# Forming a head's symmetric products once: 48 of 64 columns, three products by q, and every second head's sums begun on GpSimd

## The chip, the cores and the metric

The kernel runs on one core of a Trainium2 chip. A core has TensorE (PE, matrix products into PSUM, with weight loads PEld beside them), VectorE (DVE), ScalarE (ACT), GpSimd (POOL) and SyncE (SP, which issues DMAs). Each engine works through its own queue in order; semaphores join them. The time is device microseconds of one execution, and the median of several runs counts: 831.38 us for the kernel before (three runs, 828.76 to 834.36).

## The reference

Two transformer layers over x of 16 batches, 128 rows and 256 columns, float32, with a context of the same shape. The change touches only the first part of the first layer. For each batch, of 128 channels in 16 heads of 8 and a sequence of 256:

```python
kv = einsum('bhil,bhjl->bijhl', k_, v_)          # k_ and v_ are both the context
y = irfft(rfft(kv) * rfft(ssm_kernel))[..., :L]  # a causal convolution along l
out = y + kv * D
out = einsum('bijhl,bhil->bjhl', out, q_)        # q_ is the normed x
x = x + tanh(g_xattn[0]) * out
```

As k_ and v_ are the same tensor, kv of a head is symmetric in i and j, and so is its convolution. After it come a mixture of 8 experts beside a shared one, causal attention on the context, and a mixture of 32 experts, each added to x behind a layer norm.

## The kernel before

The convolution is done as matrix products with Toeplitz matrices. The 16 batches are two halves of 8 (`HALF`). The sequence of 256 lies on the 128 partitions in two blocks (`KC`). For a half i and a head h (16 of them, `SSM_H`), `convolve` does four things:

1. GpSimd forms `kv` (L331): for 2 blocks x 8 batches the 8 x 8 products of the head's rows, 1,024 elements a partition, in one of 2 buffers.
2. TensorE multiplies with the head's Toeplitz blocks `toe` into `y` in PSUM (L339): three matmuls of 512 columns, of block 0 for output block 0, and of both blocks for output block 1. A float32 matmul goes as two instructions, so there are six passes a head. `y` takes two of the eight PSUM banks and has 3 buffers; the two others are for transposes (`tr`).
3. VectorE multiplies `y` by the normed and transposed x, `qT` (L347), into `pr`, with i innermost (2 buffers).
4. VectorE sums over i into `qT` (L353), in the place of the head's own q.

After 16 heads TensorE transposes `qT` back (L358, tile `to`) and VectorE adds it to x (L360). The layer norm of a half is `prepare`: statistics per tile (L184, L187), the root on ScalarE (L189), its reciprocal (L190), the normalisation (L211, here with the columns reversed), transposes (L214) and a copy by ScalarE into `qT` (L216). That of the second half is woven into the heads of the first from head 6 on, held back until the product of head 5 (`meanwhile`, L362).

Behind the convolution comes the first mixture: `norm` and `choose` for chunks of four tiles (statistics again by L184 to L190, tiles `st_f`, `mv_f`, `rs_f`; rows by L211; transposes, copies `xT_f` by L216; router logits L391; Exp on ScalarE L441; the best two of 8 by L405 to L417), the shared expert (L617 into `pg` and `pu`, L431 to L433, L669 into `os`, opened by a zero product L660), then `place0` and the sends of rows to DRAM by GpSimd (L725), which are held in step with the shared expert (`paced`).

The order within each engine's queue is not the order of the source lines: the tile framework plans it when the kernel is built, by its own costs, from what each instruction needs and which buffer it takes. So a change of one stage can move instructions of the next to other places. ScalarE loads a table of functions when it changes between Sqrt, Exp and Tanh.

Of the kernel before, what the change touches and what calls it, by code (L numbers as in the profile page):

```python
# [10 lines left out]
F32 = mybir.dt.float32  # L11
# [4 lines left out]
ALU = mybir.AluOpType  # L16
AX = mybir.AxisListType

P = 128
# [8 lines left out]
TOK = CH * P  # L28

SSM_H, SSM_I = 16, 8  # L30
HALF = B // 2
# [22 lines left out]
def flamingo(ctx: ExitStack, tc: tile.TileContext, a: dict, out: bass.AP):  # L54
    nc = tc.nc
    V, S, G, T = nc.vector, nc.scalar, nc.gpsimd, nc.tensor
# [7 lines left out]
    def bank(tag, name, bufs):  # L64
        return banks[-1].tile([P, 512], F32, tag=tag, name=name, bufs=bufs)
# [127 lines left out]
    def down_from_end(t):  # L193

        return t.rearrange("p (c t) -> p c t", c=KC)[:, :, ::-1]
# [26 lines left out]
    with (  # L222
# [15 lines left out]
        for _ in range(WARM):  # L238
# [3 lines left out]
                rhs=zeros_b.unsqueeze(1).to_broadcast([P, 4, P]),  # L242
# [16 lines left out]
        for i in range(SSM_H // 4):  # L259
            at = taps[4 * i, :]  # L260
# [19 lines left out]
        at = KC * 2 * SH0 * P  # L280
# [39 lines left out]

        def convolve(i, qT, between):

            n = KC * HALF
            full = [P, n, SSM_I, SSM_I]
            q, c = (t.rearrange("p k b t -> p (k b) t") for t in (qT, cT[i]))
            for h in range(SSM_H):
                if h in between:
                    between[h](last)
                hs = slice(h * SSM_I, (h + 1) * SSM_I)
                kv = cv.tile([P, n, SSM_I, SSM_I], F32, tag="kv", name=f"kv{i}_{h}", bufs=2)  # L330
                G.tensor_tensor(  # L331
                    kv, c[:, :, hs].unsqueeze(3).to_broadcast(full), c[:, :, hs].unsqueeze(2).to_broadcast(full), ALU.mult
                )
                t = toe[h // 4][:, h % 4]
                y = cv_psum.tile([P, KC * TOK], F32, tag="y", name=f"y{i}_{h}", bufs=3)
                for lb in range(KC):
                    for kc in range(lb + 1):
                        off = P - (lb - kc) * P
                        T.matmul(  # L339
                            y[:, lb * TOK : (lb + 1) * TOK],  # L340
                            lhsT=t[:, off : off + P],
                            rhs=kv[:, kc * HALF : (kc + 1) * HALF].rearrange("p b i j -> p (b i j)"),
                            start=(kc == 0),
                            stop=(kc == lb),
                        )
                pr = cv.tile(full, F32, tag="pr", name=f"pr{i}_{h}", bufs=2)
                last = V.tensor_tensor(  # L347
                    pr,
                    y.rearrange("p (b i j) -> p b j i", b=n, i=SSM_I),
                    q[:, :, hs].unsqueeze(2).to_broadcast(full),  # L350
                    ALU.mult,
                )
                V.tensor_reduce(q[:, :, hs], pr, AX.X, ALU.add)  # L353
            for j in range(HALF):
                b = i * HALF + j
                tp = bank("tr", f"to{b}", 2)
                for lb in range(KC):
                    T.transpose(tp[:, lb * P : (lb + 1) * P], qT[:, lb, j, :], ident)  # L358
                x = xs[b].rearrange("p (c t) -> p c t", c=KC)
                V.scalar_tensor_tensor(x, down_from_end(tp[:, :D]), tg_x[:, 0:1], x, ALU.mult, ALU.add)  # L360
# [7 lines left out]
        tg_h = base.tile([P, 1], F32, tag="tg_h", name="tg_h")  # L368
        qTs = [prepare(0)]
        convolve(0, qTs[0], {6: meanwhile})  # L370
        convolve(1, qTs[1], {})

    banks.append(ctx.enter_context(tc.tile_pool(name="psum", bufs=2, space=bass.MemoryType.PSUM)))
# [634 lines left out]
    def attention():  # L1008


        chunks, sends = [], []
        for b in range(CHUNKS[-1][0]):
            if any(b == b0 for b0, _ in CHUNKS):
                steps = []
                chunks.append(steps)
            for now, before in [(0, None), (None, 2), (1, None), (None, 3), (None, 4)]:
                if now is not None:
                    steps.append(lambda b=b, i=now: part(b, i))
                elif before is not None and b > 0:
                    steps.append(lambda b=b, i=before: part(b - 1, i))  # L1020
                else:
                    continue
                if sends:
                    steps.append(sends.pop(0))
            for g in range(len(GROUPS)):
                if b > 0 and GROUPS[g][1] == b:
                    sends += dispatch(g)
        return chunks, sends
# [37 lines left out]
    chunks, left = attention()  # L1066
# [251 lines left out]
```

## Time and profile before

| | us |
|---|---|
| median of 3 runs | 831.38 |
| the profiled execution | 832.41 |
| its span, first to last instruction | 830.6 |
| convolution: first product by q to last sum over i | 21.43 to 110.25 |
| first mixture up to the first row sent | 110.3 to 137.81 |
| share of the span: PE, PEld, DVE, ACT, POOL | 85%, 60%, 65%, 44%, 40% |
| granted TensorE clock, mean | 0.919 of full speed |

A group's row in the profile reads: line, engine, operation, tiles, partitions x elements, count; then busy time in us and the mean of one in ns; then the engine's idle time before it and what ended it. A row of the timeline reads: start, length, engine, line, operation; in brackets the idle time before it and what ended that. [...] A row of a stretch gives its bounds and length, then busy time and number of instructions of PE, PEld, DVE, ACT and POOL, the granted clock, the DMA share and GB/s.

### The profile page before, as it was taken

The numbers are of one execution on the slowest core, as the hardware profiler recorded it, in microseconds if no ns is written. First come the engines' busy times: TensorE is split into PE (matmuls) and PEld (weight loads), VectorE is DVE, ScalarE is ACT, GpSimd is POOL, SyncE is SP. The second block draws the span as 40 slices with busy tenths as digits, with TensorE's granted clock in tenths as the row PEclk, the third lists the DMA queues.
The fourth block names the chain that finished last, engine by engine and source line by source line (L and its number), as shares of the span: only waits on it lengthen the run. The fifth ranks groups of instructions, "written<-read, shape, count | busy, mean of one in ns | idle before, by whom it ended". The sixth has DMA issues, their size and how long they took to land.

```text
span 830.6 us, 12160 instructions
## 1 busy us (share of the span) xinstructions
PE 703.4 (85%) x3928; PEld 496.4 (60%) x3928; DVE 541.2 (65%) x1579; ACT 367.6 (44%) x811; POOL 332.9 (40%) x326
## 2 busy tenths in 40 slices
PE   6999979989999799999969989958867999788820
PEld 3444445567775577656547747735546898677720
DVE  5999995335446754568667874685883555476756
ACT  2110037115322666652356354426524777566624
POOL 3756702300516100012272057007462677766640
PEclk8999978999999999999979987969987999999975
DMA  8999996122442233541143034063125676788575
GB/s 266 327 371 274 269 262 166 58 72 83 154 131 83 64 102 106 132 116 30 46 124 65 13 89 118 15 164 113 67 100 190 210 228 190 247 291 262 187 244 180
DMA packets 134016, 128.97 MB, mean 155 GB/s; under 512 B 42976, under 2 KB 117888, under 8 KB 133824
## 3 DMA queue, kind: packets, MB, share of 16 engines
q1 hardware_dynamic: 120704, 91.61, 39.5%
q0 software_dynamic: 13152, 36.52, 12.3%
q8 instruction: 32, 0.52, 0.3%
q14 instruction: 32, 0.26, 0.1%
q10 hardware_dynamic: 96, 0.05, 0.0%
HBM read 64.23 MB, written 63.92 MB: 154 GB/s over the span
## 4 chain that ended last, share of the span: by engine, by line
PE 46%; DVE 25%; DMA 10%; issue 7%; ACT 6%; POOL 3%; ACTq 1%; SPq 1%; DVEq 0%; POOLq 0%
PE y L339 7%; DMA part<-parts 4%; PE gu L782 4%; PE eo L1209 3%; PE sc L858 3%; PE pu L617 3%; PE pg L617 3%; PE eh L1197 3%; DVE mn L869 3%; PE eo L792 2%; PE pt L882 2%; PE os L669 2%; ACT ex L875 2%; PE avT L896 2%; PE lg_r L391 2%
## 5 line engine op out<-in xcount | busy, mean ns | idle before, releaser
L978 POOL DMA_INDIRECT sent<-row,dst x96 | 94.0, 979 | 123.8 <-DVE dst L609 94.3
L1234 POOL DMA_INDIRECT parts<-ey,to x114 | 111.6, 979 | 58.9 <-issue 23.2
L875 ACT ACTIVATE ex<-sc,mn 128x128 f32<-128x128 f32 x256 | 71.6, 385 | 68.0 <-DVE mn L869 67.9
L812 POOL DMA_INDIRECT part<-parts,places x32 | 31.2, 975 | 144.6 <-DVE rd L912 88.8
L339 PE MATMUL y<-kv,toe 128*128 128x512 f32 x192 | 85.0, 597 | 0.0
L1209 PE MATMUL eo<-wt,ehs 128*128 128x256 f32 x228 | 62.0, 403 | 17.4 <-DVE ehs L1207 17.3
L331 POOL TENSOR_TENSOR kv<-cT 128x1024 f32<-128x1024 f32 x32 | 60.6, 1893 | 38.0 <-PE y L339 33.2
L725 POOL DMA_INDIRECT sent<-row,places x32 | 31.2, 976 | 103.5 <-DVE places L504 38.2
L1187 ACT COPY wt<-wts 128x512 f32 x114 | 66.3, 620 | 13.9 <-issue 8.6
L617 PE MATMUL pg<-xT_s,wts 128*128 128x512 f32 (+1 forms) x160 | 66.3, 535 | 1.9 <-DVE silu L432 1.9
L1197 PE MATMUL eh<-xts,wt 128*128 128x128 f32 x456 | 64.7, 286 | 2.8 <-ACT wt L1187 2.8
L1197 PEld LDWEIGHTS eh<-xts,wt 128*128 128x128 f32 x456 | 62.2, 201 | 8.2 <-ACT wt L1187 4.1
L617 PE MATMUL pu<-xT_s,wts 128*128 128x512 f32 (+1 forms) x160 | 63.7, 517 | 1.9 <-DVE hs L433 1.9
L669 PE MATMUL os<-wts,hs 128*128 128x256 f32 x256 | 65.0, 387 | 0.0
L339 PEld LDWEIGHTS y<-kv,toe 128*128 128x128 f32 x192 | 36.0, 192 | 41.2 <-issue 29.1
L669 PEld LDWEIGHTS os<-wts,hs 128*128 128x128 f32 x256 | 48.4, 194 | 15.7 <-issue 9.7
L1209 PEld LDWEIGHTS eo<-wt,ehs 128*128 128x128 f32 x228 | 40.9, 197 | 25.2 <-DVE ehs L1207 20.7
L1192 DVE COPY xts<-xt 128x512 f32<-128x512 f32 x57 | 38.7, 686 | 25.5 <-PE xt L1190 18.7
L869 DVE TENSOR_REDUCE mn<-sc 128x4 f32<-128x512 f32 x64 | 41.6, 684 | 20.3 <-PE sc L858 20.0
L782 PEld LDWEIGHTS gu<-xts,wt 128*128 128x128 f32 x368 | 46.4, 196 | 8.6 <-DVE xts L776 4.8
L782 PE MATMUL gu<-xts,wt 128*128 128x128 f32 x368 | 49.2, 283 | 1.9 <-DVE xts L776 1.8
L1218 ACT COPY ey<-eo 128x512 f32<-128x512 f32 x57 | 33.4, 586 | 33.7 <-PE eo L1209 29.3
(250 smaller groups left out, 1360.0 us busy)
## 6 DMA issues: line engine op xcount, KB each, us to landing
sent<-keys SPq DMA_DIRECT2D x1, 17018.0 KB
got<-sent SPq DMA_DIRECT2D x19, 804.0 KB, 5.0
part<-parts SPq DMA_DIRECT2D x48, 256.0 KB, 4.7
sent<-keys SPq DMA_DIRECT2D x2, 2944.0 KB
got<-sent SPq DMA_DIRECT2D x22, 256.0 KB, 3.0
parts<-ey SPq DMA_DIRECT2D x22, 256.0 KB, 2.1
wts<-in_sw SPq DMA_DIRECT2D x3, 1024.0 KB, 11.8
wts<-in_w SPq DMA_DIRECT2D x3, 1024.0 KB
```

The lines of the kernel that those rows point to most:

```text
L331: G.tensor_tensor(kv, c[:, :, hs].unsqueeze(3).to_broadcast(full), c[:, :, hs].unsqueeze(2).to_broadcast(full), ALU.mult)
L339: T.matmul(y[:, lb * TOK : (lb + 1) * TOK], lhsT=t[:, off : off + P], rhs=kv[:, kc * HALF : (kc + 1) * HALF].rearrange("p b i j -> p (b i ...
L617: T.matmul(ps, lhsT=w(kc), rhs=xT[:, kc, :n], start=(kc == 0), stop=(kc == KC - 1))
L669: T.matmul(o[:, k * D : (k + 1) * D], lhsT=hs[j][:, t * P : (t + 1) * P], rhs=wC[:, j, :], start=False, stop=(j == SH0 - 1 and k == len(ts ...
L782: T.matmul(gu[:, half * D + u * P : half * D + (u + 1) * P], lhsT=wt[:, u, w : w + P], rhs=xt[:, u * D + kc * P : u * D + (kc + 1) * P], s ...
L869: least = V.tensor_reduce(mn[:, 4 * r : 4 * r + 4], scs[r].rearrange("p (h t) -> p h t", t=P), AX.X, ALU.min)
L875: S.activation(ex[:, i, :], scs[r][:, at : at + P], AF.Exp, bias=mn[:, i : i + 1], scale=-1.0)
L978: ins = G.indirect_dma_start(out=sent[:, :], out_offset=bass.IndirectOffsetOnAxis(ap=dst[:, t, k : k + 1], axis=0), in_=row, in_offset=None,)
L1187: S.copy(wt[:, i], wts[:, bass.ds(offsets[u % GRP], W1_ROW)])
L1197: T.matmul(eh[:, i * P : (i + 1) * P], lhsT=wt[:, i, cols], rhs=xt[:, i * D + kc * P : i * D + (kc + 1) * P], start=(kc == 0), stop=(kc == ...
L1209: T.matmul(eo[:, i * D : (i + 1) * D], lhsT=h[:, i * P : (i + 1) * P], rhs=wt[:, i, KC * P :], start=True, stop=True,)
L1234: ins = G.indirect_dma_start(out=parts[:, :], out_offset=bass.IndirectOffsetOnAxis(ap=to[:, t % GRP : t % GRP + 1], axis=0), in_=y[:, t % ...
```

## The change

With m = 4, the 8 x 8 products of a head fall into four blocks of 4 x 4. The block of low j and high i is the mirror of that of high j and low i, so 48 products hold all 64. `kv` now has 48 elements for each block and batch, made by two GpSimd instructions of 512 and 256 elements (all 8 rows by the high 4; the low 4 by the low 4), in 4 buffers. The matmuls take 384 columns and write 48 of every 64 columns of `y`. VectorE multiplies by q in three instructions of 512, 256 and 256 elements, the last reading the mirrored block with i and j exchanged, into a full `pr` (4 buffers). For odd heads GpSimd adds the high half of i onto the low half in `pr` (512 elements), and VectorE sums over four i in place of eight. The sum over i of a head is issued behind the products of the next head (`sums`, `add_up`).

```diff
@@ -320,37 +320,68 @@
 
         def convolve(i, qT, between):
 
             n = KC * HALF
+            m = SSM_I // 2
             full = [P, n, SSM_I, SSM_I]
             q, c = (t.rearrange("p k b t -> p (k b) t") for t in (qT, cT[i]))
+            sums = []
+            def add_up():
+                V.tensor_reduce(*sums.pop(0), AX.X, ALU.add)
             for h in range(SSM_H):
                 if h in between:
                     between[h](last)
                 hs = slice(h * SSM_I, (h + 1) * SSM_I)
-                kv = cv.tile([P, n, SSM_I, SSM_I], F32, tag="kv", name=f"kv{i}_{h}", bufs=2)
-                G.tensor_tensor(
-                    kv, c[:, :, hs].unsqueeze(3).to_broadcast(full), c[:, :, hs].unsqueeze(2).to_broadcast(full), ALU.mult
-                )
+                kv = cv.tile([P, n, 3 * m * m], F32, tag="kv", name=f"kv{i}_{h}", bufs=4)
+                k, k0, k1 = (c[:, :, hs][:, :, part] for part in (slice(0, 2 * m), slice(0, m), slice(m, 2 * m)))
+                for at, left, right in [(0, k, k1), (2 * m * m, k0, k0)]:
+                    size = [P, n, left.shape[2], m]
+                    G.tensor_tensor(
+                        kv[:, :, at : at + size[2] * m].rearrange("p b (j i) -> p b j i", i=m),
+                        left.unsqueeze(3).to_broadcast(size),
+                        right.unsqueeze(2).to_broadcast(size),
+                        ALU.mult,
+                    )
                 t = toe[h // 4][:, h % 4]
                 y = cv_psum.tile([P, KC * TOK], F32, tag="y", name=f"y{i}_{h}", bufs=3)
                 for lb in range(KC):
                     for kc in range(lb + 1):
                         off = P - (lb - kc) * P
                         T.matmul(
-                            y[:, lb * TOK : (lb + 1) * TOK],
+                            y[:, lb * TOK : (lb + 1) * TOK].rearrange("p (b s) -> p b s", b=HALF)[:, :, : 3 * m * m],
                             lhsT=t[:, off : off + P],
-                            rhs=kv[:, kc * HALF : (kc + 1) * HALF].rearrange("p b i j -> p (b i j)"),
+                            rhs=kv[:, kc * HALF : (kc + 1) * HALF],
                             start=(kc == 0),
                             stop=(kc == lb),
                         )
-                pr = cv.tile(full, F32, tag="pr", name=f"pr{i}_{h}", bufs=2)
-                last = V.tensor_tensor(
-                    pr,
-                    y.rearrange("p (b i j) -> p b j i", b=n, i=SSM_I),
-                    q[:, :, hs].unsqueeze(2).to_broadcast(full),
-                    ALU.mult,
+                pr = cv.tile(full, F32, tag="pr", name=f"pr{i}_{h}", bufs=4)
+                yb = y.rearrange("p (b s) -> p b s", b=n)
+                y01, y00 = (
+                    yb[:, :, at : at + size].rearrange("p b (j i) -> p b j i", i=m)
+                    for at, size in [(0, 2 * m * m), (2 * m * m, m * m)]
                 )
-                V.tensor_reduce(q[:, :, hs], pr, AX.X, ALU.add)
+                low, high = slice(0, m), slice(m, 2 * m)
+                for out_j, out_i, src in [
+                    (slice(0, 2 * m), high, y01),
+                    (low, low, y00),
+                    (high, low, y01[:, :, low, :].rearrange("p b j i -> p b i j")),
+                ]:
+                    dst = pr[:, :, out_j, out_i]
+                    by = q[:, :, hs][:, :, out_i].unsqueeze(2).to_broadcast(list(dst.shape))
+                    last = V.tensor_tensor(dst, src, by, ALU.mult)
+                if h % 2:
+                    G.tensor_tensor(pr[:, :, :, low], pr[:, :, :, low], pr[:, :, :, high], ALU.add)
+                    pr = pr[:, :, :, low]
+                sums.append((q[:, :, hs], pr))
+                if len(sums) > 1:
+                    add_up()
+            while sums:
+                add_up()
             for j in range(HALF):
                 b = i * HALF + j
                 tp = bank("tr", f"to{b}", 2)
```

## The prediction

> **What bounds the kernel now.** I first cut the span by stage: the convolution runs from 21.4 us (first product on VectorE) to 110.3 us (end of its last reduction). The table of busy time by stretch, columns PE, PEld, DVE, ACT, POOL, then clock and DMA:
>
> ```profile
> 21.40:66.00 44.60, 43.16 (x112) 19.35 (x111) 43.90 (x58) 4.29 (x9) 30.29 (x16) 1.00 1.01 343
> 66.00:110.30 44.30, 40.69 (x107) 18.43 (x106) 43.57 (x59) 0.20 (x1) 26.50 (x14) 1.00 1.11 269
> 110.30:138.00 27.70, 25.34 (x99) 16.16 (x100) 23.28 (x130) 14.84 (x22) 0.19 (x1) 0.69 0.92 223
> ```
>
> TensorE and VectorE are both nearly full for 88.9 us, GpSimd is not (64%). Which one sets the pace is read from the groups of this stage:
>
> ```profile
> L339 PE MATMUL y<-kv,toe 128*128 128x512 f32 x192 | 85.0, 597 | 0.0
> L331 POOL TENSOR_TENSOR kv<-cT 128x1024 f32<-128x1024 f32 x32 | 60.6, 1893 | 38.0 <-PE y L339 33.2 <-DMA cT<-in_ctxT 4.1 <-POOL kv L331 0.7
> L347 DVE TENSOR_TENSOR pr<-y,qT 128x1024 f32<-128x1024 f32 x32 | 38.6, 1213 | 5.6 <-PE y L339 5.1
> L353 DVE TENSOR_REDUCE qT<-pr 128x128 f32<-128x1024 f32 x32 | 38.1, 1208 | 0.2
> ```
>
> and from GpSimd's own order of time:
>
> ```profile
> 26.62 1.89 POOL L331 TENSOR_TENSOR kv<-cT 128x1024 f32<-128x1024 f32 x1 [0.68 <-PE y L339]
> 29.19 1.89 POOL L331 TENSOR_TENSOR kv<-cT 128x1024 f32<-128x1024 f32 x1 [0.68 <-PE y L339]
> 31.77 1.89 POOL L331 TENSOR_TENSOR kv<-cT 128x1024 f32<-128x1024 f32 x1 [0.68 <-PE y L339]
> ```
>
> The reader is to see that the products of a head start every 2.575 us and each waits 0.68 us for TensorE. The chain of waits agrees: long pieces of L339 (one of 46 matmuls, 19.76 us). 2.575 us is six passes of 0.429 us. VectorE issues L347 and L353 back to back at 1.13 us each (53.44 to 55.70 for two), so it needs 2.26 of every 2.575 us, and the layer norm of the second half (statistics, eight normalisations) and the eight updates of x eat the rest. So TensorE leads by only 12%, and VectorE is the second wall.
>
> **The change, two heads at a time** (an even and an odd one).
>
> TensorE: 12 passes over 384 in place of 512 columns. Passes of 512 go at 0.429, of 256 (L669, 8 in 1.73) at 0.216, so 384 is 0.322 and two heads take 3.87 against 5.15. Weight loads (0.19) stay hidden. The output now has gaps (48 used, 16 not), which no row shows. [...] I take 0.322, since 47 of 48 steps are contiguous. [...] At 0.429 the sum below would turn from a gain into about 5 us of loss.
>
> VectorE: intervals, not durations, count. 1024 elements take 1.13, 512 take 0.60 (L433 at 133.50, the next at 134.10), so 1.04 ns an element and 0.07 for each instruction; 256 take 0.33 (eight L211 rows, 115.57 to 118.15: 0.32 each). Products: 2 x (0.60 + 0.33 + 0.33) = 2.52 in place of 2.26, as two more instructions a head cost 0.13. Sums: 1.13 for the even head, 0.60 for the odd one, in place of 2.26. Together 4.25 against 4.52. [...] Patterns: L347 already reads y with a step of eight elements at the rate of L353, which reads without gaps, so runs of four get no surcharge. Its upper bound is L417, 1.464 us for 768 elements with a step of 32, against 0.950 for L607 without: 1.54 times.
>
> GpSimd: 1024 take 1.893, memsets of 16, 128, 512 take 0.12, 0.20, 0.517, so about 0.1 is fixed. 512 is 1.00, 256 is 0.55, kv of a head 1.55. The add of the odd head (512, both inputs full tensors) no row shows: below 0.52 (memset), above 1.54 x 1.00; I take 1.1, nearest to the 512 piece. Two heads: 2 x 1.55 + 1.1 = 4.2 against 3.79.
>
> So the three need 3.87, 4.25 and 4.2 where TensorE alone set 5.15. VectorE becomes the bound, with GpSimd 0.05 behind it.
>
> Sum for the stage. VectorE's work from first product to last reduction: 32 x 1.26 = 40.3, 16 x 1.73 = 27.7, and what stays there from the profile, 11.0 (statistics 3.1 and 0.35, normalisations 4.5 with their waits, eight x at 0.39). That is 79.0. Its start comes 0.65 earlier (six passes shorter by 0.107), at 20.8. The added wait: the reduction of an odd head h waits for GpSimd's add, and behind it in VectorE's queue stand the products of head h+2, which free the y buffer for TensorE's head h+5. In the built order the add stands behind the kv of head h+5, which waits for y of head h+1. The loop is 1.93 + 1.55 + 1.1 + 0.60 + 1.26 = 6.4 us for four heads where VectorE needs 8.5, so it does not set the pace; walking the queues head by head leaves 1.7 us of single late adds. At the very end the add (1.1) lies beside the reduction of head 14 (1.13). The stage ends at 20.8 + 79.0 + 1.7 = 101.5 in place of 110.25: **8.7 us earlier**. Four buffers instead of two are free in time.
>
> [...]
>
> ```profile
> 9.54 1.52 DVE L188 TENSOR_SCALAR rs_conv<-mv_conv 128x8 f32<-128x8 f32 x1
> 11.05 1.91 DVE L91 CAST causal_b<-causal 128x128 bf16<-128x128 f32 x1
> 9.08 1.89 POOL L331 TENSOR_TENSOR kv<-cT 128x1024 f32<-128x1024 f32 x1 [4.09 <-DMA cT<-in_ctxT]
> 10.98 1.90 POOL L331 TENSOR_TENSOR kv<-cT 128x1024 f32<-128x1024 f32 x1
> ```
>
> Two tiny instructions last until a GpSimd product ends. Products and reductions never do (1.17 to 1.22). GpSimd now works on to 15 us, beside the first normalisations, but in pieces half as long: I take nothing, with 0.7 either way.
>
> What moves. In the built order the statistics of the first half's tiles (L184, L187) no longer lie between heads: seven of eight ran from 85.5 to 109; now all stand behind the last reduction. ScalarE's second Sqrt table load, which came after the copies of the second chunk, now comes before them:
>
> ```profile
> 120.89 1.09 ACT L216 ACTIVATE xT_f<-tp_f 128x512 f32<-128x512 f32 x2 [0.29 <-PE tp_f L214]
> 122.00 1.28 ACT L189 ACT_TABLE_LOAD   x1
> 123.29 0.20 ACT L189 ACTIVATE rs_f<-rs_f 128x4 f32<-128x4 f32 x1
> ```
>
> Counted from the last reduction: the first chunk's logits come at 8.1 as before, since TensorE's opening of `os` (L660) still waits for the last x. Then Exp, the root of the first chunk's scores at 10.35, Sqrt load to 11.6, two roots to 12.05, and only then rows 4 to 7, between the pieces of the top-2 (12.4 to 14.1; before at 6.6). Their copies end at 15.3 (before 11.7), those of xT_s at 17.0 (14.2), and the logits L391 of chunk 1, on the path, start at 16.4 in place of 13.8: **2.6 us lost**, 0.5 to 4 with the reordering's doubt. Two table loads fewer later on gain nothing, as silu waits for PE there.
>
> From 138 us on SP's, GpSimd's and, but for a few places, all orders are the same, and the sends are paced by the layer beside them, so the rest shifts whole. The 17 MB fill of `sent` is through before the earlier first send (131.7): the SP queue gets on at 123.85.
>
> Sum: -8.7 + 2.6 = -6.1 us on an execution of 832.41 (span 830.6), so 826.3. That execution is 1.03 above the median 831.38; against the median it is **825.3**.
>
> **Rivals.** (1) GpSimd becomes the bound mildly, its pieces 1.05 to 1.19 times my price. For: 4.2 stands beside 4.25, and runs of four are unseen there. Two heads then take up to 5.0: the stage gains 2.4 to 6, the total lies at 828.5 to 832.5. (2) Slower: the same place beyond that point. From 1.19 times (5.0) on, 16 pairs gain less than the 2.6 lost; at 1.3 times, 5.46 a pair, the stage is 16 x 0.31 = 5.0 longer and the time 831.4 + 5.0 + 2.6 = 839; at the bound of 1.54 times 855. Against: 1.893 us hold to 0.01 for all 32. Passes at 0.429 end at 836 too. (3) Better: the reordering costs 0.5, or late adds nothing: -8.3 to -10, 820 to 823.
>
> **Numbers.** Forecast (823 to 828.5) 0.50, mild GpSimd bound 0.14, slower 0.14 (0.10 of it beyond 1%), better 0.22. About 1% (8.3 us) is what a measurement of this kernel tells from no change. Range 820 to 837: the ends of the better case and of 1.25 times, with some 0.1 left above and 0.08 below. Faster 0.22, same 0.68, slower 0.10.
>
> **What would show it.** Right: matmuls every 0.32 us, VectorE 97% busy with starts of products 2.12 us apart, the last reduction near 101.5, logits of chunk 1 some 16 us after it. [...]

## The result and the profile after

The changed kernel takes 837.75 us (median of 18 runs, 834.22 to 841.98) against 831.57 us (18 runs, 826.28 to 834.85) for the kernel before: 1.0077 times as long, 95% interval 1.0060 to 1.0094. The forecast was 825.3, its range 820 to 837. The profiled execution has a span of 838.0 us, 7.4 more than before. On two of the four chips used later ("slow chip 1" and "slow chip 2" below) every kernel, the one before included (946 and 949 us), took some 115 us longer, mostly behind 270 us; the convolution and the part behind it came out there as on the others, and a time is only set against times from the same chip. The ratios leave out executions that the record marks as slow (over 1.5% above the fastest of their kernel), and of the profiles only that of `best_noadd` is of such an execution.

In all that follows, "the convolution" is the time from VectorE's first product by q to the end of the last sum (0.08 us before the recorded end, where the next instruction starts), and "the way to the first row" the time from there to GpSimd's first send.

| profiled execution, us | before | forecast | after |
|---|---|---|---|
| first product | 21.4 | 20.8 | 20.9 |
| last sum | 110.2 | 101.5 | 108.0 |
| the convolution | 88.7 | 80.7 | 87.1 |
| the way to the first row | 27.65 | 30.3 | 33.1 |
| first row sent | 137.8 | 131.7 | 141.1 |
| shift of VectorE's work at 201, 262 us and at the end | 0 | -6.1 | +3.3, +6.4, +7.4 |

The table of busy time by stretch of the changed kernel, over the stretches that the prediction showed of before (columns PE, PEld, DVE, ACT, POOL, then clock, DMA share, GB/s):

```profile
21.40:66.00 44.60, 39.30 (x121) 22.42 (x120) 42.26 (x90) 4.29 (x9) 35.31 (x42) 0.92 1.04 346
66.00:110.30 44.30, 34.52 (x106) 18.68 (x104) 40.74 (x82) 0.00 (x0) 28.48 (x31) 0.86 1.11 262
110.30:138.00 27.70, 22.57 (x80) 15.29 (x80) 21.13 (x123) 11.79 (x19) 0.00 (x0) 0.55 0.95 230
```

The reader is to see the column behind GpSimd's. Before, TensorE's granted clock was 1.00, 1.00 and 0.69 in these stretches; now it is 0.92, 0.86 and 0.55. TensorE has less to do, and it does it more slowly. VectorE is not full, although it should now set the pace: 42.3 of 44.6 and 40.7 of 44.3.

Its groups of instructions in the convolution, each shape by itself (busy time, mean ns of one, then idle time before them and what ended it):

```profile
L355 PE MATMUL y<-kv,toe 128*128 128x384 f32 x186 | 66.7, 518 | 5.7 <-DVE pr L376 5.7
...
L344 POOL TENSOR_TENSOR kv<-cT 128x512 f32<-128x512 f32 x28 | 29.2, 1042 | 13.7 <-PE y L355 13.4 <-POOL kv L344 0.3
L376 DVE TENSOR_TENSOR pr<-y,qT 128x256 f32<-128x256 f32 x64 | 24.0, 414 | 0.0
L376 DVE TENSOR_TENSOR pr<-y,qT 128x512 f32<-128x512 f32 x32 | 21.8, 681 | 3.2 <-PE y L355 3.2
L378 POOL TENSOR_TENSOR pr<-pr 128x512 f32<-128x512 f32 x16 | 20.4, 1274 | 13.9 <-DVE pr L376 13.9
...
L334 DVE TENSOR_REDUCE qT<-pr 128x128 f32<-128x512 f32 x16 | 10.9, 681 | 4.3 <-POOL pr L378 4.2
```

The dots stand for rows left out. Here VectorE's sums wait 4.2 us for GpSimd's add, GpSimd's products wait 13.4 us for TensorE's y (a buffer of kv comes free), and its adds 13.9 us for VectorE. Each waits for the next. GpSimd at its best, in its order of time:

```profile
85.52 1.27 POOL L378 TENSOR_TENSOR pr<-pr 128x512 f32<-128x512 f32 x1
86.74 3.18 POOL L344 TENSOR_TENSOR kv<-cT 128x512 f32<-128x512 f32 x4
89.88 1.27 POOL L378 TENSOR_TENSOR pr<-pr 128x512 f32<-128x512 f32 x1
```

Without any wait two heads take it 4.36 us (85.52 to 89.88). VectorE takes 4.23 for two heads where it waits for nothing. So at its best GpSimd is the slower of the two by 0.13 us for two heads, and in this stretch VectorE's sums of odd heads start 4.36 us apart as well (86.82, 91.18).

TensorE's order of time in the changed kernel, at its two long pauses and behind them:

```profile
33.83 2.42 PE L355 MATMUL y<-kv,toe 128*128 128x384 f32 x7
39.98 4.26 PE L355 MATMUL y<-kv,toe 128*128 128x384 f32 x8 [3.73 <-DVE pr L376]
```

```profile
100.03 2.17 PE L355 MATMUL y<-kv,toe 128*128 128x384 f32 x6 [0.21 <-DVE pr L376]
108.16 1.12 PE L389 MATMUL to<-ident,qT 128*128 128x128 f32 x4 [5.96 <-DVE qT L334]
...
116.95 3.58 PE L422 MATMUL lg_r<-rw,xT_f 128*128 128x8 f32 x16
123.55 1.80 PE L214 MATMUL tp_f<-ident,row 128*128 128x128 f32 x7 [3.02 <-DVE f_e L439]
```

Ahead of the first pause seven passes take 2.42 us; behind it eight take 4.26. The record of the granted clock has it at half for 3.4 us from 39.5, for 3.4 from 49.7, for 6.8 from 70.2, and for 30.7 us in one piece from 104.3, behind the 5.96 us in which TensorE had finished its last y and VectorE had not finished its sums. The first logits (L422) take 3.58 us; in the kernel before the same sixteen took 1.99. There, too, TensorE stood before the transposes `to`, but for 3.62 us, and its record has half clock for 17.1 us of the way to the first row (two pieces, from 111.7 and from 121.9), where the changed kernel has 27.0:

```profile
110.31 0.66 PE L358 MATMUL to<-ident,qT 128*128 128x128 f32 x4 [3.62 <-DVE qT L353]
...
118.38 1.99 PE L391 MATMUL lg_r<-rw,xT_f 128*128 128x8 f32 x16
```

### The profile page after: what moved, and what is told of

It is laid out like the page before. It is cut to its first block, busy times and chain, and to the rows that moved or that the text cites. A ratio compares the mean times of both kernels' runs of the same rounds, so it can differ in the third digit from the quotient of the medians.

```text
span 838.0 us, 12272 instructions
## 1 busy us (share of the span) xinstructions
PE 690.9 (82%) x3928; PEld 497.3 (59%) x3928; DVE 539.1 (64%) x1643; ACT 364.8 (44%) x809; POOL 343.9 (41%) x374
## 4 chain that ended last, share of the span: by engine, by line
PE 42%; DVE 23%; DMA 9%; SPq 9%; ACT 6%; issue 6%; POOL 3%; ACTq 1%; DVEq 0%; POOLq 0%
SPq L304 8%; PE pu L648 4%; PE gu L813 4%; PE eo L1240 4%; PE pg L648 4%; PE os L700 3%; PE sc L889 3%; PE eh L1228 3%; DMA parts<-ey,to 3%; DVE mn L900 3%; PE eo L823 2%; PE pt L913 2%; ACT ex L906 2%; POOL parts L1265 2%; PE avT L927 2%
## 5 line engine op out<-in xcount | busy, mean ns | idle before, releaser
L1265 POOL DMA_INDIRECT parts<-ey,to x114 | 111.9, 981 | 61.1 <-ACT ey L1249 30.3
L843 POOL DMA_INDIRECT part<-parts,places x32 | 31.2, 976 | 144.5 <-DVE rd L943 88.8
L355 PE MATMUL y<-kv,toe 128*128 128x384 f32 x192 | 69.5, 521 | 5.7 <-DVE pr L376 5.7
L1218 ACT COPY wt<-wts 128x512 f32 x114 | 66.3, 620 | 13.5 <-issue 9.6
L1228 PE MATMUL eh<-xts,wt 128*128 128x128 f32 x456 | 63.0, 282 | 1.9 <-ACT wt L1218 1.8
L344 POOL TENSOR_TENSOR kv<-cT 128x512 f32<-128x512 f32 x64 | 51.3, 830 | 17.7 <-PE y L355 13.4
L355 PEld LDWEIGHTS y<-kv,toe 128*128 128x128 f32 x192 | 38.0, 205 | 34.7 <-issue 8.2
```

The costliest lines, as they stand in the source:

```text
L355: T.matmul(y[:, lb * TOK : (lb + 1) * TOK].rearrange("p (b s) -> p b s", b=HALF)[:, :, : 3 * m * m], lhsT=t[:, off : off + P], rhs=kv[:, k ...
L1218: S.copy(wt[:, i], wts[:, bass.ds(offsets[u % GRP], W1_ROW)])
L1228: T.matmul(eh[:, i * P : (i + 1) * P], lhsT=wt[:, i, cols], rhs=xt[:, i * D + kc * P : i * D + (kc + 1) * P], start=(kc == 0), stop=(kc == ...
L1265: ins = G.indirect_dma_start(out=parts[:, :], out_offset=bass.IndirectOffsetOnAxis(ap=to[:, t % GRP : t % GRP + 1], axis=0), in_=y[:, t % ...
```

## The experiments

Fifteen runs, in the order of the argument. Ratios are to the kernel before on the same chip (`after5`, `noadd`, `late` and `best` share one, `after_c`, `fill3` and `stats_fill3` another); "clock" is the mean granted clock from 104 to 135 us (0.72 in the kernel before, 0.51 in the first profile of the changed one).

| run | ratio (95%) | convolution | way to the first row | clock |
|---|---|---|---|---|
| again (slow chip 1) | 1.0135, one run | 87.4 | 33.2 | 0.52 |
| after5 | 1.0081 (1.0056 to 1.0106) | 86.8 | 33.2 | 0.51 |
| after_c | 1.0094 (1.0062 to 1.0125) | 86.2 | 33.3 | 0.52 |
| addfree (slow chip 1) | 0.9993 (0.9962 to 1.0025) | 80.1 | 33.5 | 0.59 |
| noadd | 1.0046 (1.0021 to 1.0072) | 86.8 | 33.2 | 0.51 |
| gap (slow chip 2) | 1.0017 (0.9981 to 1.0053) | 82.7 | 33.6 | 0.56 |
| fill (slow chip 1) | 0.9983 (0.9951 to 1.0015) | 84.7 | 30.9 | 0.89 |
| fill3 | 0.9962 (0.9941 to 0.9982) | 84.1 | 31.4 | 0.83 |
| stats (slow chip 1) | 1.0020 (0.9986 to 1.0053) | 89.9 | 27.4 | 0.67 |
| stats_fill3 | 0.9901 (0.9869 to 0.9933) | 86.5 | 24.6 | 1.00 |
| late | 1.0055 (1.0026 to 1.0084) | 84.7 | 29.9 | 0.68 |
| best | 0.9872 (0.9823 to 0.9921) | 82.9 | 24.6 | 1.00 |
| best_nofill (slow chip 2) | 0.9897 (0.9846 to 0.9949) | 83.2 | 27.5 | 0.69 |
| best_noadd (slow chip 2) | 0.9899 (0.9845 to 0.9952) | 87.2 | 28.9 | 0.83 |
| oldbest (slow chip 2) | 0.9972 (0.9938 to 1.0006) | 91.5 | 24.6 | 1.00 |

### The changed kernel again: again, after5, after_c

> The changed kernel once more, for a second profile. Its first profile showed a span of 838.0 us against 830.6: last reduction of the convolution at 108.0 (before 110.25), first row sent at 141.1 (137.8), and a further 3.0 us lost near 218-228, where VectorE's copy into a row buffer waited 5.4 us for a send to land (4.1 before), TensorE stood 2.1 us and then ran 3.4 us at half clock. If stage and tail follow from the program, they come back to within 0.3 us. If the loss at 218 is chance, it goes and the span is near 835; if it follows from the new places of the sends, it comes back and the span is near 838.

> The changed kernel timed beside the others of this set. From the result, 1.0077 times the kernel before (1.006 to 1.0094); a single execution beside the first set stood at 1.0135. Theory that stages and not chance carry the loss: again a convolution of 87 us, 33 us from the last reduction to the first row, a third loss of 1.5 to 3 us between 212 and 235, and a ratio between 1.005 and 1.014 on any chip.

> The changed kernel timed beside the two: convolution 86.8 to 87.4 us, 33.1 us to the first row, 1.005 to 1.014 of the kernel before.

In four profiles of the changed kernel the convolution took 86.2 to 87.4 us and the way to the first row 33.1 to 33.3. So both come back; how far the length of the convolution hangs on chance all the same, `late` shows below. In the three on the usual chips VectorE's work also slipped by another 3.0 to 3.2 us between 201 and 262 us; `again`, on slow chip 1, slipped 1.7 us more there. That is no sign of the change: on the slow chips other kernels slip there too, `oldbest` by 6.7 us.

### Without the add: addfree, noadd

```diff
-                    G.tensor_tensor(pr[:, :, :, low], pr[:, :, :, low], pr[:, :, :, high], ALU.add)
```

> The changed kernel without GpSimd's add: VectorE sums only the low four i of the odd heads, so half of their products are left out of the sums. GpSimd then needs 3.1 us for two heads in place of 4.36, VectorE 4.24 as before. Theory of the late adds: VectorE's 4.3 us of waits for them go, the last reduction comes near 103.7 in place of 108.0, and the time falls by 4 us to about 834. Rival, that VectorE has the next wait ready (TensorE's y, or the order in the queues): the stage gets less than 1.5 us shorter. Third theory, of the clock: whatever the stage gains, TensorE still runs dry before the last reduction, and the way from the last reduction to the first row sent stays at 33 us.

```diff
-                if h % 2:
-                    G.tensor_tensor(pr[:, :, :, low], pr[:, :, :, low], pr[:, :, :, high], ALU.add)
-                    pr = pr[:, :, :, low]
```

> The changed kernel without GpSimd's add; VectorE sums all eight i of every head, so nothing is left out. VectorE pays 16 x 0.54 = 8.7 us more for sums. Theory that the waits the add brings cost nearly what it saves: leaving it out wholly shortened the convolution from 87.4 to 80.1 us, so here it is 80.1 + 8.7 = 88.8, 1.4 us longer than with the add. Rival, the price list of the prediction, by which the add saves all but 1.7 us: 94 us, 7 longer. The way from the last reduction to the first row stays at 33 us in both.

`addfree` leaves the high four i of odd heads out of their sums. Without the add the convolution is 7.3 us shorter (87.4 to 80.1) where its waits were 4.1, and the way to the first row stays (33.5). That is within 1.1 us of the work that the prediction had for VectorE (79.0). Not all of the 7.3 us is the add's: half clock ahead of TensorE's last y fell from 13.7 to 3.4 us as well. Against `fill3`, which has the add and as much half clock, the difference is 4.0 us (84.1). In `noadd` VectorE does the add's work itself, 8.7 us of it, and the convolution is as long as with the add (86.8 against 86.2 to 87.4): in the changed kernel the add gains next to nothing there. Both lengths in that expectation were too long (88.8 and 94). Why a wait that the prediction put at 1.7 us costs 4 to 7 is what the next run asks.

### TensorE kept busy in its first pause: gap

The edit, shortened, with comments added:

```diff
+                if (i, h) == (0, 5):
+                    keep_busy(ins, FILL[0], "fill0")   # FILL[0] = 16 products of zeros, 512 columns, bf16
+                if (i, h) == (0, 8):
+                    queue(held[0], ins)                # the first of them behind y of head 8
...
+                        if (i, h, lb) == (0, 9, 0):
+                            queue(ins, held[-1])       # y of head 9 behind the last of them
```

> The changed kernel with 16 products of zeros by zeros (3.5 us) on TensorE behind y of head 8 of the first half, where it stands idle for 3.7 us (from 36.2) while VectorE forms the second half's statistics; nothing else, nothing left out. In three profiles of the changed program half clock followed at 39.5, 49.7 and 70.2 us (13.6 us in all) and the convolution took 86.8 to 87.4 us; in one profile of a program with the same order there it fell to 6.8 us in one piece, and the convolution took 84.7. Theory of the clock: no half clock between 35 and 60, waits for GpSimd's add below 2 us in place of 4.1, convolution 83.5 to 85 us, time 2 to 4 us under the changed kernel's, about 834.5. Rival, VectorE and GpSimd set the pace whatever TensorE's clock: 86.8 to 87.4 us and 837.5.

The convolution falls from 87.1 to 82.7 us, by 4.4, though nothing useful was added; of the useful work only eight transposes of `tp_conv` on TensorE and one product on GpSimd changed places, near 42 to 47 us. TensorE's order of time in this run, at the place of the first pause:

```profile
33.71 2.42 PE L373 MATMUL y<-kv,toe 128*128 128x384 f32 x7
35.97 3.62 PE L327 MATMUL fill<-zeros_b 128*128 128x512 bf16 x16
39.87 2.17 PE L373 MATMUL y<-kv,toe 128*128 128x384 f32 x6 [0.29 <-DVE pr L400]
```

Head 9 starts when it did (39.87, in the changed kernel 39.98), but its six passes take 2.17 us, where eight had taken 4.26. The group of the odd heads' sums in this run:

```profile
L352 DVE TENSOR_REDUCE qT<-pr 128x128 f32<-128x512 f32 x16 | 10.8, 673 | 2.1 <-POOL pr L402 2.1
```

The waits for the add are 2.1 us in place of 4.2 (the expectation had them below 2). In this pair half of them went with the half clock: y was late, kv's buffers came free late (GpSimd waits 9.0 us for y in place of 13.4), and the add stands behind those products in GpSimd's queue. The waits alone don't follow the half clock from run to run, though: `late`, below, has 6.8 us of it and waits 2.1 us, and `best`, with another order, has none and waits 3.5. The way to the first row is as long as ever, 33.6 us, as the second pause (5.96 us) is still there. The time is 1.0017 (0.9981 to 1.0053) on slow chip 2, where the changed kernel wasn't timed; so what `gap` gains in time isn't shown.

### TensorE kept busy in its second pause, and in both: fill, fill3

The edit of `fill`, shortened, with a comment added; `fill3` has that of `gap` as well:

```diff
+                fill = bank("tr", "fill", 2)
+                for _ in range(28):                    # behind the last y of the second half, ahead of `to`
+                    ins = T.matmul(..., lhsT=zeros_b, rhs=zeros_b..., start=True, stop=True)
+                    queue(ins, filled)
+                    filled = ins
```

> The changed kernel with 28 products of zeros by zeros (512 columns, bf16, 0.216 us each at full clock, 6.0 us) on TensorE behind the last y of the second half, where it stood idle for 6 us. Theory of the clock: without the idle time the clock is not halved from 104 to 135 us in one piece but only as in the kernel before (mean 0.7 in place of 0.55 from the last reduction to 138 us), the first logits take 2.0 in place of 3.6 us, and the first row leaves 2 to 3 us earlier; time about 835. Rival, that TensorE's speed is hidden there: clock higher, first row at 33 us after the last reduction as before, time 837.5. A second rival: the products of zeros last longer than the idle time and hold up the transposes; then the stage behind is up to 3 us later.

> The changed kernel with products of zeros by zeros in both places where TensorE stood idle: 16 behind y of head 8 of the first half, 28 behind the last y; nothing else, nothing left out. Filling the first alone gave a convolution of 82.7 us (87.1 before it), filling the second alone a way of 30.9 us from the last reduction to the first row (33.1). Theory that the idle clock carries the loss: both together, 82.7 to 83.5 us and 30 to 31 us, first row at 134 to 135 us in place of 141; time 6 us under the changed kernel timed beside it and level with or a little under the kernel before (0.995 to 1.002). Rival, that the two gains overlap or are given back behind the first row: at most 3 us under the changed kernel.

With the second pause filled, the way to the first row is 30.9 us and the time 0.9983. The planned order behind the last sum moved as well: the rows of the second chunk now come before the first scores, its logits 16.0 us after the last sum in place of 19.1, and ScalarE loads a table three times on the way in place of five. So the 2.2 us gained there are clock and order together. The convolution was shorter too (84.7), which this edit can't do, as the queues are the same up to there: the half clock fell otherwise in that execution, in one piece of 6.8 us from 39.1 in place of three.

With both filled (`fill3`), beside the changed kernel on one chip, 1.0094 becomes 0.9962 (0.9941 to 0.9982): 839.4 us to 827.6. Forty-four products that compute nothing take 11.8 us off a kernel that had lost 7.8; by their two intervals it is 8 to 14 us, an estimate. The profiled executions differ by 7.5 us: VectorE's work is 5.9 us earlier at 200 us and 8.0 at 262. The expectation's 6 us was too low for the medians; its level, 0.995 to 1.002, was met; its stages were not (84.1 us where 82.7 to 83.5 were expected, 31.4 for 30 to 31, the first row at 136.4 for 134 to 135). So the loss hangs on TensorE's two pauses. How much of the gain is the clock by itself these two runs can't say, since the order behind the last sum and the places of the sends moved too; the pairs of profiles under `late` can.

### The first half's statistics ahead of the last sums: stats, stats_fill3

Of the edit, the calls alone:

```diff
-        convolve(1, qTs[1], {})
+        convolve(1, qTs[1], {4: two_stats(0), 6: two_stats(2), 8: two_stats(4), 10: two_stats(6), 12: root, 14: invert})
```

> The changed kernel with the first half's layer-norm statistics, their root and its reciprocal between heads 4 to 14 of the second half, as far as order goes; nothing left out. Theory of the order: the normalisations of all eight tiles can follow the last update of x, so logits of chunk 1 come 14 to 15 us after the last reduction in place of 19.1, the first row is sent some 28 us after it in place of 33.0; VectorE, being full, makes the stage 3.2 us longer, so the time falls by 1 to 2.5 us to about 836. Theory of the clock alone: half speed of TensorE and not the order fills the tail, the first row leaves not earlier than 32 us after the last reduction, and the time rises by 2 to 3 us to about 840.

> As the run before, with the first half's statistics, root and reciprocal between heads 4 and 14 of the second half as well; nothing left out. Theory of two parts: VectorE, which sets the pace, pays 3.2 us in the convolution (86 us), and the order gives 2.4 us or more beyond the clock: 24.6 us to the first row, as in the fastest kernel; first row at 131 to 132 us, time 2 to 3 us under the run before. Rival, that the order gains only what the half clock had cost: 27.5 us and no gain against the run before.

With only the order changed, the way to the first row is 27.4 us, as before the change (27.65), and VectorE pays 2.5 us in the convolution. The stretch from 104 to 135 us, first of the changed kernel, then of `stats`:

```profile
104.00:135.00 31.00, 22.41 (x80) 15.70 (x81) 25.71 (x132) 11.79 (x19) 1.27 (x1) 0.51 1.03 253
```

```profile
104.00:135.00 31.00, 22.98 (x91) 15.08 (x90) 26.49 (x122) 12.97 (x19) 2.54 (x2) 0.67 1.00 246
```

The clock has changed too (0.51 to 0.67): with the work sooner, TensorE's wait of 3.0 us behind the first logits is gone (none above 0.6 us is left there behind the pause of 6.0), so order and clock are not apart here. With the pauses filled as well (`stats_fill3`) the way is 24.6 us, as the first theory had it, and the time 0.9901, 5.4 us under `fill3` beside it, where 2 to 3 were expected.

### A copy that waits for a send: late

```diff
-            V.tensor_scalar_add(row[:, D : D + TOPK1], expert[:, t, :TOPK1], 1.0)
-            V.tensor_copy(row[:, D + TOPK1 :], places[:, b0 + t, :])
+            ins = V.tensor_scalar_add(row[:, D : D + TOPK1], expert[:, t, :TOPK1], 1.0)
+            queue(V.tensor_copy(row[:, D + TOPK1 :], places[:, b0 + t, :]), ins)
```

What the expectation speaks of, in the changed kernel's order of time, on VectorE and on TensorE:

```profile
222.25 0.17 DVE L1007 COPY row<-places 128x6 f32<-128x6 f32 x1 [5.39 <-DMA sent<-row,places]
```

```profile
223.25 1.15 PE L823 MATMUL eo<-wt,h 128*128 128x256 f32 x3 [2.13 <-DVE h L464]
```

> The changed kernel with VectorE's copy of places into a row buffer held behind the copy of the expert's number into that row, in the queue alone; nothing left out. That copy had waited 5.4 us for a send's landing near 217 to 222, and a hidden layer's product behind it made TensorE wait 2.1 us. Theory that this wait carries the third loss: the 1.7 to 3.0 us between 212 and 235 go, and all behind is 1.5 to 3 us earlier. Rival, that the sends' pace or the half clock has them: nothing changes by more than 0.5 us there. First row sent at 141 to 142 as before in both.

The copy of six numbers into a row buffer that is still being sent holds up VectorE for 5.39 us (before the change 4.09), TensorE stands 2.13 us (0.83), and half clock follows for 3.4 us from 223.8. In `late` TensorE waits 0.5 us there, and VectorE's work is 1.1 us ahead of the kernel before at 200 us and 2.2 ahead at 240: the loss is gone there. But `noadd` and `stats_fill3` have none either (2.96 to 3.05 and -6.55 to -6.46 between 200 and 262), without this edit. So the wait's length hangs on where the sends fall. In time, `late` has 835.45 us against 837.87 for the changed kernel beside it, with overlapping intervals; that part is not settled by times.

`late` shows something else by accident, and it is the cleanest evidence for the clock. Up to 195 us the queues of TensorE, VectorE, ScalarE and GpSimd are those of the changed kernel, instruction for instruction, but in its profile the half clock fell otherwise: 6.8 us in one piece in the convolution, and 20.5 us in place of 30.7 behind it. The same part of the program took 84.7 and 29.9 us in place of 87.1 and 33.1. Up to the logits of the second chunk both are at half clock and level (19.1 us behind the last sum); these logits and all behind them gain the 3.2 us. First the changed kernel, then `late`:

```profile
127.16 3.55 PE L422 MATMUL lg_r<-rw,xT_f 128*128 128x8 f32 x16
```

```profile
124.11 1.95 PE L422 MATMUL lg_r<-rw,xT_f 128*128 128x8 f32 x16
```

Eight profiles have this convolution (`after` is the first of the changed kernel). In the first six the four engines have the same queues there, in the last two those of `gap`. Its length follows the half clock that fell ahead of TensorE's last y:

| | after | again | after5 | after_c | late | fill | fill3 | gap |
|---|---|---|---|---|---|---|---|---|
| half clock, us | 13.7 | 13.7 | 13.7 | 10.2 | 6.8 | 6.8 | 3.4 | 0 |
| convolution, us | 87.1 | 87.4 | 86.8 | 86.2 | 84.7 | 84.7 | 84.1 | 82.7 |

### All of it, and its parts: best, best_nofill, best_noadd, oldbest

`best` has the early statistics of `stats`, the 28 products of `fill`, the copy held back, and, in place of the lump of statistics that made the first pause, two tiles' statistics a head, with the normalisations on ScalarE (shortened):

```diff
-        convolve(0, qTs[0], {6: meanwhile})
+        convolve(0, qTs[0], {4: next_stats(0), 5: next_stats(2), 6: next_stats(4), 7: next_stats(6), 8: next_root, 9: next_norm})
...
+                    S.activation(xn..., down_from_end(xs[...]), AF.Identity, bias=nb_1[...], scale=rs_1[...])
```

> Everything together, nothing left out: the changed kernel with the first half's statistics, root and reciprocal between heads 4 and 14 of the second half; the second half's statistics two tiles a head from head 4 on in place of one lump, its eight normalisations on ScalarE; 28 products of zeros on TensorE behind the last y; the copy of places held back. Theory that VectorE and the order behind it set the pace: VectorE loses 5.3 us of normalisations and their waits and 1 us of a wait for GpSimd, pays 3.2 for the first half's statistics: the convolution takes 84 us, the first row follows 27 us after the last reduction at 132 to 133 (before 137.8), no third loss: 4 to 6 us faster than the kernel before. Rival, that GpSimd is the bound and gives back what VectorE saves: a convolution of 87 us, 1 to 2 us faster than before.

> The fastest kernel so far (819.3 us, 0.987 of before) without its 28 products of zeros behind the last y; nothing left out. There the first row followed 24.6 us after the last reduction, with no half clock from 20 to 169 us; in the kernel before it was 27.65, with 17 us of half clock. Theory of the clock: TensorE stands 6 us again, half clock of 10 to 20 us comes back behind it, first row 27 to 28 us after the last reduction, time about 822.5. Rival, the order alone gave those 3 us: 24.6 us, time 819.

> The fastest kernel so far without GpSimd's add: VectorE sums all eight i of every head; nothing left out. VectorE pays 8.7 us more and loses 3.2 us of waits for the add. Theory that the add is worth its saving once TensorE's clock holds: convolution 82.9 + 5.5 = 88.4 us, time 824 to 825. Rival, as in the changed kernel without the add (86.8 against 86.8 to 87.4 us, time 3 us less): no difference or a gain, time at most 820.

> The kernel before, with its 64 products, one product by q and two buffers, but with the same four repairs as in the fastest kernel: the second half's normalisations on ScalarE and its statistics spread, the first half's statistics between the heads, 17 products of zeros behind the last y, the copy of places held back. Theory that TensorE binds it and the 48 products are worth something once the rest is repaired: the convolution takes 32 x 2.575 + 2 = 84.5 to 86 us (before 88.7, changed and repaired 82.9), the first row 25 us after it, time 822 to 824. Rival, that the repairs alone carry the gain: convolution at most 83.5 us, time at most 820.

`best` takes 819.31 us, 0.9872 (0.9823 to 0.9921) of the kernel before: faster than both, and by more than expected. The stretch from 104 to 135 us of `best`, then of `best_nofill`:

```profile
104.00:135.00 31.00, 27.46 (x124) 16.40 (x123) 22.31 (x126) 14.59 (x23) 5.03 (x5) 1.00 1.07 268
```

```profile
104.00:135.00 31.00, 28.04 (x107) 18.29 (x108) 23.93 (x127) 16.74 (x23) 2.46 (x3) 0.69 1.02 252
```

Taking the 28 products out brings half clock back (1.00 to 0.69), and the way to the first row goes from 24.6 to 27.5 us. These 2.9 us are again clock and order together: the planned order moved, with seven table loads on the way in place of three and the logits of the second chunk 13.9 us after the last sum in place of 11.0. `best_noadd` needs 87.2 us for the convolution in place of 82.9, with no half clock in either, so by these two profiles the add is worth 4.3 us there; in time this can't be told (0.9899, and 0.9897 for `best_nofill` on the same chip). `oldbest`, the old convolution with the same repairs, needs 91.5 us for it, far from the 84.5 to 86 that were expected, and is level with the kernel before at 0.9972, though its way to the first row is as short as that of `best`. Two tiny VectorE instructions beside GpSimd's long products last 1.7 and 1.8 us there; what else makes it long is not shown. On the same chip `best_nofill` has 83.2 us and 0.9897 (0.9846 to 0.9949; that of `oldbest` is 0.9938 to 1.0006). So the 48 products seem worth their place once TensorE's clock and the order behind are looked after: the convolutions say so, the times nearly.

## Why the prediction was wrong

Point by point, by its own steps:

- **TensorE, 0.322 a pass**: right at full clock, 2.17 us for the six passes of a head with the last one's length. The starts are 0.32 apart, three quarters of 0.429, so the gaps of 16 in the output, between runs of 48 columns, cost nothing in these matmuls.
- **VectorE, 4.25 for two heads**: right, 4.23. The products of 512 elements step at 0.60 and those of 256 at 0.33 (they are 0.68 and 0.41 long), as the prediction took them from L433 and L211 of the kernel before. That they read y in runs of four cost nothing beside these steps.
- **GpSimd, 4.2**: 4.36 measured. A head's products take 1.57 and the add 1.22 from start to start, against 1.55 and 1.1: 1.04 times the price. That turns the order of the two bounds round: GpSimd is not 0.05 behind VectorE but 0.13 slower. The mild rival was to begin at 1.05, though by the prediction's own 4.25 GpSimd is ahead from 1.01 on. The size is small: in `gap`, where GpSimd is as slow, VectorE's waits for the add are 0.4 us above the forecast.
- **The stage, 79.0 + 1.7**: this step failed. The account of the convolution on VectorE:

| us | forecast | after | gap |
|---|---|---|---|
| products | 40.3 | 40.9 | 40.4 |
| sums | 27.7 | 27.9 | 27.7 |
| waits for the add | 1.7 | 4.3 | 2.1 |
| the rest | 11.0 | 14.0 | 12.5 |
| sum | 80.7 | 87.1 | 82.7 |

With TensorE's clock held (`gap`) the sum is 2.0 off, by the waits 0.4, the rest 1.5 (0.9 of it is the small instruction beside GpSimd, below) and the products 0.1. What the forecast had no term for is TensorE's clock: 4.4 us between these two profiles, 2.4 between `after` and `late`, which have the same queues. The forecast took TensorE, once it was no longer the bound, as free and as fast as before. But TensorE had stood for 3.73 us, the next 3.4 us ran at half speed, and then a head takes longer than VectorE's 2.12 us: eight passes took 4.26 us, which is 3.2 for six.

- **The small instruction beside GpSimd, "nothing, 0.7 either way"**: VectorE's step ahead of the root (L188, eight numbers) lasts until a GpSimd piece ends:

```profile
38.43 1.07 DVE L188 TENSOR_SCALAR rs_conv<-mv_conv 128x8 f32<-128x8 f32 x1
```

GpSimd's pieces end at 39.47, this at 39.50. Four such numbers take 0.16 us elsewhere (at 113.69), so it costs 0.9 us, a little outside the bound.
- **The way to the first row, "+2.6, 0.5 to 4"**: the order changed as told, but +5.5 was measured, and the logits of chunk 1 came 19.1 us after the last sum where 16.4 was forecast. The prediction took the stretch's clock of 0.69 as given. On the way itself `late` had the changed kernel's order with 19.0 us of half clock and took 29.9 us; `stats`, with the statistics early as in the kernel before, had 18.0 us of it and took 27.4, the kernel before 17.1 us and 27.65. By these totals the order cost 2.3 to 2.5 us and the longer half clock 3.2 (33.1 against 29.9, 27.0 us of it against 19.0). That the first comes so near to 2.6 is partly luck: the half clock lies at other places in the three, and up to the logits order and clock together cost 5.2 us (19.1 against 13.9).
- **"The rest shifts whole"**: wrong by 4.1 us. 3.1 fall at the wait of one copy for a send: TensorE waits 1.3 us longer there, and 3.4 us of half clock behind it are worth some 1.7 (an estimate: half of 3.4). Why the wait is longer stays open. 1.0 comes later and is no more than chance: behind 262 us `after5` and `after_c` are 3.1 and 1.5 us faster than the kernel before.
- **The rivals**: the slower one gave 836 and more, where the time fell, but by GpSimd's price from 1.19 times on. That was not what happened; no rival named the clock. VectorE did stand idle on GpSimd's add, for 4.3 us, as it would with GpSimd as the bound; but at 1.04 times its price GpSimd explains little of it, and with the half clock gone (`gap`) half of these waits went.

In sum, -6.1 was forecast and +7.4 came: 6.5 in the convolution, 2.9 on the way to the first row, 4.1 behind it. Some 7.6 of these 13.5 us are half clock in the first two places (4.4 by `gap`, 3.2 by `late`), and filling both pauses gave back 11.8 us of the time, with the order moved too. So the step that failed is the overlap: TensorE, with less to do, was taken to be covered by VectorE at no cost and at the clock that it had before.

## What to carry to other kernels

Where an edit takes work from the engine that sets the pace, ask what that engine does in the time it gains: if it is TensorE, and it stands as here for 3.7 or 6.0 us, its next work can run at half clock (here for 3.4 and 30.7 us), and a chain that was covered is not covered any more. Look for the places where it will have little to do (a lump of other work on VectorE, the end of a stage) and spread that lump, bring the next stage's work forward, or fill the pause with products of zeros. And a helper engine's add that stands behind its own late work isn't free (here 4.3 us of waits where 1.7 were forecast): price it with the queue that it stands in.

## What the runs showed of the hardware

In the profiles of the kernel before (15 pieces) and of the changed kernel (16) TensorE's half clock comes in pieces of 3.41 us and is all or half: every piece is 3.4, 6.8, 10.2 us and so on, but for the last, which runs into the end of the profile. Within each of these two profiles all pieces start on one grid of that step: in the changed kernel's first profile 39.5, 49.7, 70.2 and 104.3 lie 8, 11, 17 and 27 steps behind the first piece at 12.2. It set in inside the pauses of 3.73 and 5.96 us, at 39.5 and 104.3; with sixteen products of zeros in the first pause there was none of it in `gap` from 35 to 100 us, and in `fill3` 3.4 us from 70.6.

Half clock came without a long pause as well. The pieces at 49.7 and 70.2 follow 3.4 us in which TensorE was busy for 1.8 us (1.83 from 46.32, 1.77 from 66.80), with short transposes and no pause above 0.93 us. Nor did it end as soon as work came back: from 104.3 to 135.0 us TensorE was busy for 22.4 of 30.7 us, with pauses of 0.2 to 3.0 us behind the long one, and stayed at half; from 124.82 to 131.65, two whole steps, the profile has TensorE busy throughout, and half clock lasted to 135.0. What starts a piece and what ends it is not shown beyond these cases.

The grid lies otherwise from profile to profile (the first piece at 12.67 us in the kernel before, at 12.17 in the changed one), and the same queues gave 13.7 us of half clock ahead of TensorE's last y in one profile and 6.8 in another, and 87.1 and 84.7 us. In these profiles the length of the two stages thus varied by 2.4 us (87.1 and 84.7) and 3.2 us (33.1 and 29.9).
